# A grouped convolution, a LoRA feed-forward layer and a residual on one core: W loaded behind the first rows, shared factors cast as 96 rows, another order in the last pair

## The chip, the core and the metric

The kernel runs on one NeuronCore of a Trainium2 chip. The metric is the device time of one execution in microseconds (us); lower is better. Five engines run their own queues of instructions in order and wait for each other by semaphores: PE (matrix multiply; PEld is its weight load), DVE (elementwise, the only engine besides ACT that reads matmul results here), ACT (elementwise, casts), POOL (elementwise, in SBUF only) and SP, which here issues most of the DMAs. ACT issues the others.

## The reference

Everything is float32. Cut to what is computed, with x of 64 samples x 64 channels x 1024:

```python
# convolution over the last axis, 4 groups of 16 channels, width 9
y = conv(x, weight, pad=4, groups=4) + (cond @ c_weight.T)[:, :, None] + fside[None, :, None]
# feed-forward on rows of 1024; 8 batches, each with its own mixture of 16 LoRAs of rank 32
base  = y @ kernel + bias
A_eff = einsum('bn,nri->bri', gate, lora_A)
B_eff = einsum('bn,nor->bor', gate, lora_B)
delta = (y @ A_eff.T) @ B_eff.T + (y @ A_shared.T) @ B_shared.T
out = x + base + delta
```

## The kernel before, in words

**Precision.** PE multiplies in a reduced float32 format. Each operand is split in two: a cast on ACT gives the high part (steps whose names end in `hi`) and a subtraction gives the low part (`lo`, on DVE, or on POOL where the step carries `p`). A product is three matmuls: high x high, high x low, low x high.

**Tiles.** The 4096 rows form 16 pairs, p = 0 to 15, of 256 rows. A pair's input comes as 4 groups g (`xload p g`, 258 KB each). For pairs 0 to 2 a group is convolved by `conv` (six matmuls of 512 columns). From pair 3 on a form with fewer multiplications is used: `xdiff` (two halves), `xohi`/`xolo`, `xdhi`/`xdlo` prepare it, `convo` (3) and `convd` (6 matmuls of 256 columns) do it, `evmid` (ACT) and `evac` (DVE) take the result from PSUM. `turned` transposes it on DVE into `z`, with the rows' features on the partitions.

**Products.** Pairs 0 and 1 multiply plainly: `plain p b k` is three matmuls of output block b (2 x 2 blocks of 128 x 512) and slice k of 8. Pairs 2 to 15 use a seven-product scheme (Strassen's, in Winograd's form) on quarters of the rows and of W: `prod p j`, 12 matmuls each, for

    PRODUCTS = ((A11, B11, "a"), (A12, B21, "a"), (S1, T1, "d"), (S3, T3, "c"), (A22, N4, "c"), (S2, T2, "b"),
                (S4, B22, "d"))

The third entry is the PSUM bank in which the product is summed; there are five such banks in turn, which `fmm` and `mix` also use. `keep` (ACT) copies a bank that later products go on adding to, so the next product into that bank waits for it. `asum` (POOL) forms the sums S; `yhi`/`ylo` split an operand. `xsum`, `ysum`, `radd`, `yadd` and `total` (DVE, some on POOL) put products together with the residual rows of `rload`, and `store` writes one block of 256 KB, issued by ACT.

**W.** `wload k h` brings one of 16 pieces (256 KB, two DMAs). `fmm` multiplies the shared LoRA factors, `fadd` adds that to W, so that the shared LoRA costs the rows nothing. `whi`/`wlo` split the pieces; `wsum` forms the T and N sums for the seven-product scheme. The shared factors come by `saload`/`sbload`, 32 rows each, and are cast twice into a tile of 96 rows (two high parts, one low part: `sahi`, `salo`, `sbhi`, `sblo`).

**LoRA of a batch.** `lload`, `mix`, `mixout`, `mixput` mix the 16 factors by the gate and write them to DRAM; `aload`/`bload` read a batch's factors; `lora` multiplies a pair's rows by A, `axlow`, `axsum`, `axhi`, `axlo` split the result, and `delta` (one matmul for each block) adds B's part and the bias.

**Order.** The order of the work is written out by hand, as a long list of steps in `ORDER` (lines 50 to 246). A loop at the end of the kernel calls each step's function in that order, and each engine gets its instructions in the order in which the steps issue them; nothing reorders them later. So a step in the list sets the place of its instructions in every queue that it uses, its DMAs' place in SP's or ACT's queue too.

**Names for the lines of the profile.** L266 is any cast to a high part, L271 any subtraction for a low part; L319 is `conv`, L327 `xdiff`, L347 `convo` and `convd`, L365 `evmid`, L377/L379 `evac`, L388 `turned`, L413 `asum`, L475 `fmm`, L479 `fadd`, L485 `wsum`, L580 `plain`, L592 `prod`, L602 `lora`, L636 `keep`, L641 `xsum`, L649 `radd`, L653 `yadd`, L660 `delta`, L666 `total`, L669 `store`. In tile names `xd` is the split of a convolution's differences, `xo` that of its odd columns, `y` that of a product's operand, `wl` a low part of W, `s` a sum of `asum`, `r` the residual rows.

Of the kernel before, what the change touches and what calls it, by code (L numbers as in the profile page):

```python
# [10 lines left out]
ALU = mybir.AluOpType  # L11
# [14 lines left out]
DS = 3 * R  # L26
# [36 lines left out]
fmm 1 1, fadd 0 0, yhi 1 0, conv 2 0, wload 7 1, xlo 2 1 v, whi 0 0, fadd 0 1, biput 1, conv 2 1, whi 7 0,
fadd 1 0, wlo 0 0 p, mixput 0 0, xhi 2 2, wlo 7 0 v, mixput 0 1, whi 0 1, plain 0 0 0, fadd 1 1, xhi 2 3,
mixput 0 3, plain 0 1 0, xlo 2 2 v, whi 7 1, fmm 2 0, wlo 0 1 v, mixput 0 2, plain 0 2 0, wlo 7 1 v,
plain 0 0 1, xload 3 0, fadd 2 0, xload 3 1, fmm 2 1, plain 0 3 0, fadd 2 1, ylo 1 0 p, yhi 1 7, whi 0 2,
fmm 3 0, evac 2 0, xlo 2 3 p, whi 7 2, plain 0 3 1, wlo 0 2 v, conv 2 2, fadd 3 0, wlo 7 2 v, fmm 3 1, whi 0 3,
plain 0 0 2, fadd 3 1, plain 0 3 2, twsum, rload 0 0, whi 7 3, fmm 4 0, wlo 0 3 v, rload 0 1, plain 0 1 1,
thi 1, rload 0 2, tlo 1 v, plain 0 0 3, fadd 4 0, rload 0 3, plain 0 1 2, wlo 7 3 v, whi 1 0, fmm 4 1,
plain 0 2 1, fadd 4 1, plain 0 1 3, wsum 2 3 v, whi 6 0, plain 0 3 3, wlo 1 0 v, yhi 1 1, wlo 6 0 v, fmm 5 0,  # L70
plain 0 2 2, fadd 5 0, plain 0 1 4, ylo 1 1 v, whi 1 1, fmm 5 1, ylo 1 7 v, plain 0 0 4, aload 0, fadd 5 1,
plain 0 2 3, xohi 3 0, xdiff 3 0 0 v, whi 6 1, fmm 6 0, wlo 1 1 v, plain 0 3 4, yhi 1 4, fadd 6 0,
xdiff 3 0 1 p, plain 0 2 4, xohi 3 1, ylo 1 4 v, fmm 6 1, plain 0 0 5, fadd 6 1, xolo 3 1 p, plain 0 2 5,
wlo 6 1 v, lload 1 0, lload 1 1, lload 1 2, whi 1 2, whi 6 2, fmm 7 0, wlo 1 2 v, plain 0 3 5, wlo 6 2 v,
lload 1 3, lload 1 4, lload 1 5, lload 1 6, plain 0 2 6, fadd 7 0, xolo 3 0 p, lora 0, wsum 2 2 v, whi 1 3,
xload 3 2, wsum 2 1 v, fmm 7 1, axlow 0, turned 2 0, plain 0 1 5, evac 2 1, wsum 2 0 p, plain 0 3 6,
turned 2 1, wsum 3 0 p, conv 2 3, fadd 7 1, axsum 0, plain 0 0 6, whi 6 3, wlo 1 3 v, axhi 0, lora 1, axlo 0,
xdhi 3 0, wlo 6 3 v, lload 1 7, evac 2 2, plain 0 2 7, axlow 1, turned 2 2, wsum 3 2 p, plain 0 0 7, axsum 1,
aload 1, plain 0 1 6, total 0 0, xdlo 3 0 p, axhi 1, plain 0 3 7, evac 2 3, xdiff 3 1 0 p, plain 0 1 7,
turned 2 3, yhi 2 0, xdiff 3 1 1 p, convo 3 0, total 0 3, yhi 2 1, asum 2 3, convd 3 0, xload 3 3, evmid 3 0 a,  # L80
total 0 2, lora 2, ylo 2 1 v, xdhi 3 1, asum 2 2, xohi 3 2, evac 3 0, mix 1 0, axlow 2, xdlo 3 1 v, mix 1 1,
mixout 1 0, xdiff 3 2 0 v, mixput 1 0, mix 1 2, xdiff 3 2 1 v, mixout 1 1, turned 3 0, xolo 3 2 p, mixput 1 1,
plain 1 0 0, axsum 2, mixout 1 2, ylo 2 0 v, mix 1 3, mixput 1 2, total 0 1, plain 1 0 1, wsum 3 1 v,
xload 4 0, mixout 1 3, wsum 5 1 v, plain 1 1 0, mixput 1 3, wsum 4 1 v, plain 1 2 0, plain 1 1 1, wsum 3 3 v,
wsum 5 3 v, plain 1 3 0, wsum 4 3 v, plain 1 2 1, plain 1 1 2, wsum 5 0 v, bload 0 0, wsum 4 0 v, plain 1 2 2,
wsum 5 2 v, plain 1 3 1, bload 0 1, whi 2 0, wlo 2 0 v, whi 2 1, plain 1 1 3, wlo 2 1 v, whi 2 2, plain 1 3 2,
wlo 2 2 v, whi 2 3, plain 1 1 4, wlo 2 3 v, whi 3 0, bhi 0 0, plain 1 2 3, wsum 4 2 v, plain 1 1 5, blo 0 0 v,
bhi 0 1, plain 1 2 4, wlo 3 0 v, whi 3 1, delta 0 0 1, blo 0 1 v, plain 1 1 6, total 0 0 1, plain 1 2 5,
wlo 3 1 v, whi 3 2, store 0 0, delta 0 1 1, wlo 3 2 v, whi 3 3, plain 1 2 6, total 0 1 1, plain 1 0 2,
wlo 3 3 v, bload 1 0, whi 4 0, store 0 1, delta 0 2 1, plain 1 0 3, wlo 4 0 v, whi 4 1, plain 1 2 7,  # L90
total 0 2 1, rload 1 0, delta 0 3 1, wlo 4 1 v, whi 4 2, store 0 2, plain 1 0 4, axhi 2, total 0 3 1,
plain 1 1 7, wlo 4 2 v, store 0 3, prod 2 0, rload 1 1, whi 4 3, axlo 2, axlo 1, wlo 4 3 v, bload 1 1, whi 5 0,
rload 1 2, plain 1 0 5, yhi 2 3, rload 1 3, keep 2 0, delta 1 2 0, ylo 2 3 v, plain 1 0 6, asum 2 5,
delta 1 1 0, plain 1 0 7, total 1 1, plain 1 3 3, store 1 1, total 1 2, prod 2 3, yhi 2 2, ylo 2 2 v,
store 1 2, wlo 5 0 v, whi 5 1, asum 2 6, wlo 5 1 v, delta 1 0 0, yhi 2 4, rload 2 0, plain 1 3 4, bhi 1 0,
convo 3 1, total 1 0, whi 5 2, plain 1 3 5, rload 2 2, blo 1 0 v, store 1 0, convd 3 1, xohi 3 3, ylo 2 4 v,
keep 2 3, plain 1 3 6, xolo 3 3 v, xdhi 3 2, wlo 5 2 v, prod 2 4, evmid 3 1 a, xdlo 3 2 v, whi 5 3,
xdiff 3 3 0 v, evac 3 1, xdiff 3 3 1 p, turned 3 1, rload 2 1, xload 4 1, convo 3 2, yhi 2 5, plain 1 3 7,
evmid 3 2 a, ylo 2 5 v, convd 3 2, yhi 2 6, delta 1 3 0, xdhi 3 3, evac 3 2, convo 3 3, prod 2 1, evmid 3 3 a,
total 1 3, ylo 2 6 p, turned 3 2, store 1 3, bhi 1 1, xdlo 3 3 v, xohi 4 0, blo 1 1 v, xohi 4 1, wlo 5 3 v,  # L100
convd 3 3, yhi 3 0, xdiff 4 0 0 v, bload 2 0, prod 2 2, ylo 3 0 v, xdiff 4 0 1 v, xolo 4 0 v, rload 2 3,
xdhi 4 0, evac 3 3, xolo 4 1 p, xload 4 2, turned 3 3, prod 2 5, xdlo 4 0 v, keep 2 2, asum 3 3, yhi 3 1,
ysum 2 v, asum 3 2, ylo 3 1 v, delta 2 0, yhi 3 3, prod 2 6, total 2 0, xdiff 4 1 0 p, xsum 2, store 2 0,
xdiff 4 1 1 p, radd 2 2 v, delta 2 2, yhi 3 2, xload 4 3, convo 4 0, convd 4 0, evmid 4 0 a, radd 2 1 v,
lora 3, radd 2 3 v, xdhi 4 1, yadd 2 v, xohi 4 2, total 2 2, xolo 4 2 p, prod 3 0, rload 3 0, axlow 3,
evac 4 0, store 2 2, turned 4 0, xdlo 4 1 p, axsum 3, ylo 3 3 v, axhi 3, delta 2 1, axlo 3, delta 2 3,
asum 3 5, keep 3 0, convo 4 1, total 2 1, convd 4 1, xohi 4 3, total 2 3, store 2 1, prod 3 1, rload 3 2,
store 2 3, xdiff 4 2 0 v, xdiff 4 2 1 v, evmid 4 1 a, ylo 3 2 v, xload 5 0, xdhi 4 2, evac 4 1, xolo 4 3 p,
yhi 3 4, turned 4 1, xdlo 4 2 p, convo 4 2, yhi 3 5, ylo 3 4 v, prod 3 3, rload 3 1, evmid 4 2 a, asum 3 6,
xdiff 4 3 0 v, rload 3 3, xdiff 4 3 1 v, convd 4 2, keep 3 3, ylo 3 5 v, xload 5 1, convo 4 3, xdhi 4 3,  # L110
evac 4 2, prod 3 2, evmid 4 3 a, aload 2, turned 4 2, xdlo 4 3 p, yhi 3 6, xohi 5 0, ylo 3 6 v, xdiff 5 0 0 v,
xdiff 5 0 1 v, xohi 5 1, convd 4 3, xolo 5 0 v, keep 3 2, xolo 5 1 v, xload 5 2, prod 3 4, yhi 4 0, evac 4 3,
xdhi 5 0, turned 4 3, ysum 3 p, ylo 4 0 v, asum 4 3, xdlo 5 0 v, prod 3 5, yhi 4 1, asum 4 2, ylo 4 1 v,
# [136 lines left out]
def adaln_ffn(ctx: ExitStack, tc: tile.TileContext, xt, x, tw, w0, w1, w2, la, lb, gt,  # L250
# [164 lines left out]
    def yhi(p, b):  # L415
        if p == 1 and b in (A11, A21):
            spl[p, b] = [slot("c", f"y{q}{b}_{p}", (P, HK, P), F32R) for q in "hl"]
        else:
            t = slot("y", f"y{b}_{p}", (P, 2, HK, P), F32R)
            spl[p, b] = (t[:, 0], t[:, 1])  # L420
# [387 lines left out]
```

## Time and profile before

| | us |
|---|---|
| median of 3 runs | 467.26 (466.52 to 469.9) |
| the profiled execution, its own time | 469.12 |
| its span in the profile | 467.3 |
| busy in the span: PE / DVE / ACT / POOL | 451.1 / 415.5 / 246.2 / 213.9 |
| PEld (weight loads, beside PE) | 361.7 |

The span runs from the program's first to its last instruction; the execution's own time is 1.8 us longer. Busy times are of one engine each, and they overlap. PE's granted clock was 1.0 nearly throughout (mean 0.995). The chain of waits that ended last lies for 51% of the span on PE and for 29% on DVE. DMA engines moved 66.5 MB, at 231 GB/s in the first 10 us and 289 in the next, and at 142 over the span.

### The profile page before, as it was taken

How to read it: one execution, taken by the hardware profiler on the slowest of the kernel's cores; microseconds unless marked ns; L12 is line 12 of the kernel's file. 1: busy time of each engine (PE TensorE's matmuls, PEld its weight loads, DVE VectorE, ACT ScalarE, POOL GpSimd, SP SyncE). 2: the span in 40 equal slices, each digit the busy share in tenths (PEclk: the TensorE clock that was granted, in tenths of full speed). 3: DMA queues.
4: the chain of work that ended last, by engine and by line, in shares of the span. 5: the costliest groups of instructions: out<-in, count | busy, mean ns of one | idle time of the engine just before them, and what ended most of it. 6: DMA issues, size and time to landing. Idle time of an engine off the chain costs nothing.

```text
span 467.3 us, 7701 instructions
## 1 busy us (share of the span) xinstructions
PE 451.1 (97%) x2562; PEld 361.7 (77%) x2562; DVE 415.5 (89%) x630; ACT 246.2 (53%) x605; POOL 213.9 (46%) x181
## 2 busy tenths in 40 slices
PE   8799899999999998999999999999999999999995
PEld 7467666688888886888888888888888888888784
DVE  5799999978999879999999999998999989998734
ACT  4774354556473735556363655556363655656220
POOL 2370451022657454554546455573566553563500
PEclk9899999999999999999999999999999999999999
DMA  8999825353452625335362434335344434433232
GB/s 225 308 279 231 262 56 125 130 172 128 142 169 70 204 56 161 123 91 177 98 198 69 161 101 159 125 91 175 100 148 115 165 102 157 125 91 130 69 113 90
DMA packets 52087, 66.52 MB, mean 142 GB/s; under 512 B 6096, under 2 KB 33744, under 8 KB 52048
## 3 DMA queue, kind: packets, MB, share of 16 engines
q1 hardware_dynamic: 42112, 49.18, 36.6%
q10 hardware_dynamic: 9936, 16.86, 9.9%
q8 instruction: 20, 0.33, 0.3%
q14 instruction: 19, 0.16, 0.1%
HBM read 47.13 MB, written 18.87 MB: 141 GB/s over the span
## 4 chain that ended last, share of the span: by engine, by line
PE 51%; DVE 29%; issue 8%; DMA 5%; ACT 4%; SPq 2%; POOL 1%; DVEq 0%; ACTq 0%; POOLq 0%
PE mm_c L592 12%; PE mm_a L592 9%; PE mm_d L592 8%; PE mm_b L592 5%; PE cv L347 4%; DVE r L666 4%; DVE y L271 3%; DVE xd L271 3%; DVE xf L327 3%; DVE r L649 2%; DVE v L379 2%; PE cm L347 2%; DVE wl L271 2%; DVE bst L271 2%; PE mm_a L580 2%
## 5 line engine op out<-in xcount | busy, mean ns | idle before, releaser
L592 PE MATMUL mm_a<-wh,y 128*128 128x512 f32 x224 | 76.7, 403 | 1.4 <-ACT c L636 1.0
L592 PE MATMUL mm_d<-wh,y 128*128 128x512 f32 x224 | 75.0, 395 | 0.0
L592 PE MATMUL mm_c<-wh,y 128*128 128x512 f32 x224 | 74.8, 395 | 0.0
L266 ACT CAST y<-s 128x512 fp32r<-128x512 f32 x56 | 35.1, 626 | 67.0 <-PE mm_b L592 25.9
L271 POOL TENSOR_TENSOR xd<-xf,xd 128x512 fp32r<-128x512 f32 x21 | 27.6, 1316 | 61.8 <-ACT xd L266 61.8
L365 ACT ACTIVATE md<-cm,cadd 128x64 f32<-128x64 f32 x208 | 48.3, 317 | 12.8 <-DVE y L271 8.8
L592 PEld LDWEIGHTS mm_a<-wh,y 128*128 128x128 f32 x224 | 42.1, 188 | 13.7 <-ACT c L636 2.4
L592 PEld LDWEIGHTS mm_d<-wh,y 128*128 128x128 f32 x224 | 42.2, 188 | 9.5
L592 PEld LDWEIGHTS mm_c<-wh,y 128*128 128x128 f32 x224 | 42.0, 188 | 9.1
L388 DVE STREAM_TRANSPOSE z<-v 128x512 f32<-128x512 f32 x64 | 45.6, 712 | 2.1
L347 PE MATMUL cv<-xd,th 128*128 128x256 f32 x208 | 45.8, 282 | 1.3 <-POOL xd L271 0.8
L592 PE MATMUL mm_a<-wl,y 128*128 128x512 f32 x112 | 44.3, 396 | 0.0
L592 PE MATMUL mm_d<-wl,y 128*128 128x512 f32 x112 | 44.3, 395 | 0.0
L592 PE MATMUL mm_c<-wl,y 128*128 128x512 f32 x112 | 44.2, 395 | 0.0
L266 ACT CAST xd<-xf 128x512 fp32r<-128x512 f32 x52 | 32.6, 627 | 21.2 <-DVE xf L327 16.0
L271 DVE TENSOR_TENSOR y<-s,y 128x512 fp32r<-128x512 f32 x48 | 32.9, 686 | 11.2 <-ACT y L266 10.8
L327 DVE TENSOR_TENSOR xf<-xt 128x256 f32<-128x256 f32 x73 | 41.8, 597 | 0.8
L271 DVE TENSOR_TENSOR y<-z,y 128x512 fp32r<-128x512 f32 x38 | 40.1, 1057 | 0.9 <-ACT y L266 0.7
L266 ACT CAST y<-z 128x512 fp32r<-128x512 f32 x48 | 29.9, 623 | 18.9 <-PE mm_c L592 18.3
L413 POOL TENSOR_TENSOR s<-s,z 128x512 f32<-128x512 f32 x14 | 19.6, 1399 | 44.0 <-DVE y L271 43.0
L379 DVE TENSOR_TENSOR v<-cv,md 128x512 f32<-128x512 f32 x52 | 35.5, 683 | 4.0 <-ACT md L365 2.4
L347 PEld LDWEIGHTS cv<-xd,th 128*128 128x128 f32 x208 | 35.5, 188 | 3.3 <-DVE xd L271 1.1
(154 smaller groups left out, 1062.0 us busy)
## 6 DMA issues: line engine op xcount, KB each, us to landing
xt<-in_dram SPq DMA_DIRECT2D x64, 258.0 KB, 3.2
r<-in_dram SPq DMA_DIRECT2D x64, 256.0 KB, 3.3
out_dram<-r ACTq DMA_DIRECT2D x64, 256.0 KB, 3.4
ls<-in_dram SPq DMA_DIRECT2D x16, 256.0 KB, 5.3
br<-eff SPq DMA_DIRECT2D x48, 64.0 KB, 2.3
wr<-in_dram SPq DMA_DIRECT2D x16, 176.0 KB, 3.9
eff<-ls SPq DMA_DIRECT2D x16, 128.0 KB, 2.4
wr<-in_dram SPq DMA_DIRECT2D x16, 80.0 KB, 3.6
```

Of the source, the lines that this page charges most:

```text
L266: nc.scalar.copy(dst, src)
L271: engs[eng].tensor_tensor(dst, src, f32(hi), ALU.subtract)
L327: engs[eng].tensor_tensor(xdf[p, g][:, e], m, odd(p, g), ALU.subtract)
L347: nc.tensor.matmul(ps, a[:, w, g, :], b, start=(n == 0), stop=(n == 2))
L365: nc.scalar.activation(t[:, n], cpm[p, g][:, n], ACTF.Identity, bias=c[:, n:n + 1])
L379: nc.vector.tensor_tensor(v.rearrange("p n (i e) -> p e n i", e=2), cps.pop((p, g)), mid.pop((p, g)).unsqueeze(1).to_broadcast([P, 2, 4, H ...
L388: nc.vector.transpose(z[:, :, :, :, gg, :], vs.pop((p, g)).rearrange("p m j -> p (m j)"))
L413: engs[eng].tensor_tensor(t, m, n, op)
L580: nc.tensor.matmul(acc[p, BLOCKS[b]], m[:, kk, :], n, start=(k == 0 and q == 0), stop=(k == 7 and q == 2))
L592: nc.tensor.matmul(ps, a[:, k, :], b[bb, k], start=s, stop=(k == HK - 1 and q == 2), skip_group_check=not first)
L649: engs[eng].tensor_tensor(r, r, cop[p, "x"], ALU.add)
L666: nc.vector.tensor_tensor(r, acc[p, (BLOCKS[b], b)[of]], r, ALU.add)
```

## The change

- **Front of the order.** One of the two tap loads, pair 0's rows and the shared factors are loaded first, then W's first piece, pair 1's and most of pair 2's rows, and the rest of W. All LoRA loads (`lload`) move behind W, and `mix` behind the start of pair 0's products. Pair 0's products start after pair 0's convolutions and the first two of pair 1; before, they started after those of pairs 0 and 1 and two of pair 2. Three evacuations (`evac 0 0`, `1 0`, `1 3`) go from DVE to ACT.
- **Shared factors.** The host lays them out three times over 96 rows in both kernels. Before, 32 of these rows were loaded and cast twice; now all 96 are loaded (192 KB instead of 64) and cast by one instruction, and the low part is taken from rows of the same partitions.
- **Pairs.** Among the steps on DVE and POOL, 16 `xdiff`, 19 `xdlo`, 18 `xolo` and 3 `ysum` (net, of the whole kernel) go from POOL to DVE, and 15 `ylo` from DVE to POOL. `lora` of the next pair and its first product now come ahead of the following pair's first convolution, and each group's convolution shifts accordingly.
- **Last pair.** Its products go 0, 2, 1, 5, 3, 4, 6 instead of 0, 3, 1, 2, 4, 5, 6. Block 1, which is last, is totalled in two halves of 256 columns (`totalh`), which are stored by SP and by ACT (`storeh`).
- `yhi` gets a condition on PLAIN, which is 2 in both.

The number and shape of PE's instructions stay the same. The diff, with the list of steps cut to its beginning and end:

```diff
 ORDER = """
-twload 0, gload, warm, busy 22, twload 1, cwload, xload 0 0, ctload, xload 0 1, small 0, xload 0 2, small 1,
-xload 0 3, lload 0 0, lload 0 1, thi 0, saload 0, sbload 0, tlo 0 v, thi 2, saload 1, cwide, sbload 1, tlo 2 v,
-lload 0 2, xhi 0 0, cmul, lload 0 3, xlo 0 0 v, xload 1 0, xhi 0 1, gmask, xload 1 1, conv 0 0, xload 1 2,
-csum, bihi, xload 1 3, xlo 0 1 v, biput 0, evac 0 0, xhi 0 2, conv 0 1, lload 0 4, lload 0 5, turned 0 0,
...
+warm, twload 0, small 0, busy 22, xload 0 0, gload, twload 1, cwload, xload 0 1, ctload, saload 0, small 1,
+sbload 0, saload 1, sbload 1, thi 0, xload 0 2, xload 0 3, tlo 0 v, xhi 0 0, wload 0 0, xlo 0 0 v, thi 2,
+wload 0 1, cwide, xload 1 0, tlo 2 v, xhi 0 1, cmul, xload 1 1, xlo 0 1 v, xload 1 2, sahi 0, conv 0 0, gmask,
+xload 1 3, sbhi 0, xload 2 0, csum, sahi 1, xload 2 1, salo 0 v, conv 0 1, xload 2 2, sbhi 1, sblo 0 v,
+wload 1 0, bihi, salo 1 v, evac 0 0 a, fmm 0 0, wload 1 1, sblo 1 v, xhi 0 2, turned 0 0, wload 2 0, fmm 0 1,
...
-yhi 15 5, ylo 15 5 v, rload 15 1, rload 15 3, prod 15 2, yhi 15 6, ylo 15 6 v, prod 15 4, keep 15 2, ysum 15 v,
-prod 15 5, delta 15 0, xsum 15, prod 15 6, total 15 0, radd 15 1 v, store 15 0, radd 15 3 v, radd 15 2 v,
-delta 15 2, delta 15 1, yadd 15 v, delta 15 3, total 15 2, total 15 1, store 15 2, total 15 3, store 15 1,
-store 15 3
+yhi 15 4, ylo 15 4 v, rload 15 2, rload 15 3, prod 15 5, yhi 15 6, ylo 15 6 v, delta 15 0, xsum 15, prod 15 3,
+total 15 0, radd 15 1 v, store 15 0, radd 15 2 v, radd 15 3 v, delta 15 3, keep 15 3, delta 15 1, prod 15 4,
+ysum 15 v, yadd 15 v, total 15 3, store 15 3, prod 15 6, delta 15 2, totalh 15 1 0, total 15 2, storeh 15 1 0,
+totalh 15 1 1, store 15 2, storeh 15 1 1
 """

     def yhi(p, b):
-        if p == 1 and b in (A11, A21):
+        if PLAIN == 2 and p == 1 and b in (A11, A21):

     def saload(h):
-        sar[h] = piece(f"sar{h}", (R, HN))
-        nc.sync.dma_start(sar[h], las[0:R, HN * h:HN * h + HN])
+        sar[h] = piece(f"sar{h}", (DS, HN))
+        nc.sync.dma_start(sar[h], las[:, HN * h:HN * h + HN])

     def sahi(h):
         sa[h] = piece(f"sa{h}", (DS, HN), F32R)
-        hi_of(sa[h][0:R], sar[h])
-        hi_of(sa[h][R:2 * R], sar[h])
+        hi_of(sa[h], sar[h])

     def salo(h, eng="v"):
-        engs[eng].tensor_tensor(sa[h][2 * R:3 * R], sar[h], f32(sa[h][0:R]), ALU.subtract)
+        d = sa[h][2 * R:3 * R]
+        lo_of(d, sar[h][2 * R:3 * R], d, eng)
...
+    def totalh(p, b, c):
+        s = slice(c * HN // 2, (c + 1) * HN // 2)
+        r = res[p, b][:, s]
+        nc.vector.tensor_tensor(r, acc[p, BLOCKS[b]][:, s], r, ALU.add)
+
+    def storeh(p, b, c):
+        n = HN // 2
+        (nc.sync, nc.scalar)[c].dma_start(xrow(out, p, b)[:, :, c * n:c * n + n], res[p, b][:, c * n:c * n + n])
```

`sbload`, `sbhi` and `sblo` change as `saload`, `sahi` and `salo` do.

## The prediction

> **What bounds the kernel now.** I read the totals first (PE is busy 451.1 us of a 467.3 us span), then busy time by stage. The four stages run from the first convolution (7.1 us) to pair 1's first product (72.1), to pair 3's first (124.5), through eleven alike pairs (to 415.7), and to the last matmul.
>
> ```profile
> core 0: us, PE busy (x) PEld busy (x) DVE busy (x) ACT busy (x) POOL busy (x), PEclk, DMA share, GB/s
> 7.10:72.10 65.00, 59.14 (x320) 39.69 (x319) 60.29 (x91) 36.83 (x72) 29.74 (x23) 0.97 0.78 224
> 72.10:124.50 52.40, 51.66 (x265) 40.65 (x263) 47.12 (x74) 27.02 (x60) 10.75 (x9) 1.00 0.48 143
> 124.50:415.70 291.20, 288.50 (x1721) 238.75 (x1717) 273.46 (x410) 161.66 (x428) 158.00 (x132) 1.00 0.42 130
> 415.70:461.70 46.00, 46.00 (x241) 37.20 (x237) 30.35 (x51) 17.39 (x42) 14.41 (x11) 1.00 0.28 97
> ```
>
> PE looks full, but its ends are modelled, so I count what it issues. The chain of waits prices the pieces: 2.80 us for a product's 12 matmuls (0.233 each), 0.35 and 0.71 for the two parts of a late convolution, 1.01 for a `lora`.
>
> ```profile
> 253.13 2.81 PE mm_d L592 x12
> 255.94 0.23 PE mm_c L660
> 256.17 0.35 PE cm L347 x3
> 256.52 0.71 PE cv L347 x6
> 257.23 1.01 PE axp L602 x32
> ```
>
> A pair is 7 x 2.80 + 4 x 1.06 + 4 x 0.233 + 1.01 = 25.75 us. Stage 3 is 11 pairs, 283.3 us of work in 291.2: 7.9 lost. Stage 1 holds 12 first-form convolutions (1.40 each), 16 `fmm` (0.235), 7 `mix` (0.96), 3 `lora`, 32 `plain` (0.70) and one late convolution: 53.7 us in 65.0, so 11.3 lost. Stage 2 loses 1.9, stage 4 0.3. So 21 us of issue time are to be had, over half at the front.
>
> Third, rows by form on DVE and POOL, to see who makes PE wait.
>
> ```profile
> L327 DVE TENSOR_TENSOR xf<-xt 128x256 f32<-128x256 f32 x73 | 41.8, 597 | 0.8
> L271 DVE TENSOR_TENSOR y<-z,y 128x512 fp32r<-128x512 f32 x38 | 40.1, 1057 | 0.9 <-ACT y L266 0.7
> ...
> L271 DVE TENSOR_TENSOR y<-s,y 128x512 fp32r<-128x512 f32 x48 | 32.9, 686 | 11.2 <-ACT y L266 10.8
> ...
> L271 DVE TENSOR_TENSOR xd<-xf,xd x31: 648/725/1822, 70.3 to 424.2; 128x512 fp32r<-128x512 f32 x31
> L271 POOL TENSOR_TENSOR xd<-xf,xd x21: 1272/1302/1527, 63.6 to 427.8; 128x512 fp32r<-128x512 f32 x21
> ```
>
> The last two lines give shortest, median and longest. The same subtraction takes DVE 0.65 us or up to 1.82, and the difference is about one POOL operation (1.3). Over their shortest, five groups lose 50 us: `xf` 12, `y<-z` 15, `xd` 15, `wl` 5, the first `r` addition 3. That is about 0.25 us per us of POOL's 213.9. The Trainium skill (SBUF — State Buffer, Who interferes with whom) says that a DVE operation with two SBUF inputs and a GpSimd one that reads SBUF hold a shared port in turn, and the loser waits in full.
>
> **The change, part by part.** DVE steps are counted at their back-to-back spacing: 0.60 us for 128x512 (three radds in 1.89), 0.635 for a transpose, 0.335 for 256 columns, 0.55 for an `axsum`.
>
> *Front.* Ahead of pair 0's first product, DVE had 24 full steps, 8 transposes, 3 short ones and the mask (0.46) = 21.0 us of work, and the product began at 32.2: 11.2 us above its work. Now it has 17, 4, 2 and the mask = 13.9, since pair 1's convolutions follow the first W. DVE cannot begin before its first loaded data (5.1), so the product begins between 19.0 and 25.1. I take 21.9, the 8.0 between. The first W tile now stands behind 2.3 MB on SP instead of 4.4; at the 231 GB/s that moved in the first 10 us and the 289 in the next, plus 2.4 us to land, it is there near 13.5 instead of 20.4. The last W (9.0 MB deep) is in by 36 and is needed after 50. `saload`/`sbload` carry 192 KB for 64 and pass groups 2 and 3 of pair 0's rows, which now end 2.05 and 2.31 MB deep: they land near 11.3 and 12.4 us instead of 8 and 9. Bare, that is 3.4 us; the bounds on the start contain it. Eight ACT casts become four (2.5 us less), but all four wait for the wider loads, and `evac 0 0` (0.95 us on ACT for 0.6 on DVE) and the next `xhi` queue behind them: the value 8.0 rather than 5.1.
>
> From there to pair 1's first product DVE had 33.2 us of work and took 39.9, with 17.5 us of POOL beside it. Now it has 39.0 (pair 0's T and N sums come forward) with 11.6 us of POOL: 4.4 us extra in proportion, 6.7 if it stays, 5.0 taken. So 21.9 + 39.0 + 5.0 = 65.9. PE's work up to there is 48.3 (two `lora`, one `mix` and two convolutions later), so it loses 65.9 - 7.1 - 48.3 = 10.5, against 11.3: **gain 0.8**, from -4.1 (start 25.1, extra 6.7) to +4.3 (start 19.0, extra 4.4).
>
> *Stage 2.* PE has 54.9 us, DVE 42.0 plus at most 6: PE sets it. The named gaps of before are two single-bank `delta` waits and two of 0.28 behind `mix`; the same bank pattern stays, and `mix` now also takes turns with `fmm` in the spare bank. Loss 0.5 to 2.5, taken 1.5 against 1.9: **gain 0.4**. `aload 0` and eight `mixput` issues move behind W; the `lora 0` that needs them waits behind 32 products.
>
> *Pairs.* 32 steps net leave POOL in these 11 pairs: 11 `xdiff`, 18 `xdlo`, 13 `xolo`, 3 `ysum` go to DVE and 13 `ylo` come. POOL falls by 29 us to 129; DVE rises from 215.1 to 253 x 0.60 + 44 x 0.635 + 122 x 0.335 + 11 x 0.55 = 226.7. With 0.25 per POOL us: 254.6 before, 259.0 after, under PE's 283.3. The rows thus say +4.4 on DVE, hidden by 2.2 us of slack per pair. By the skill's exclusive lock alone each POOL us removed could free up to one, 29 - 11.6, and DVE would fall by 17.
>
> The gaps of before that are named are few:
>
> ```profile
> PE mm_a L592 <- ACT c L636: 1.0, 2, 0.8
> ...
> PE cv L347 <- POOL xd L271: 0.8, 1, 0.8
> ```
>
> Both sit at 180-183, where a convolution waited for POOL's `xdlo` and the next product for `keep`. With `xdlo` on DVE that goes, but later `xdlo` now queue behind `evac` and the transpose, 1 us before the convolution needs them: one POOL collision (1.2 us) is late. **Gain 1.5**, from -5 (0.5 more per pair) to +5.
>
> *End.* PE's last issue is at 461.51, the last store lands 4.8 us later: three totals, three issues, three blocks on one queue.
>
> ```profile
> 463.03 0.68 DVE L666 TENSOR_TENSOR r<-mm_b,r 128x512 f32<-128x512 f32 x1
> ...
> 462.55 1.88 ACTq L669 DMA_DIRECT2D out_dram<-r  x3
> ...
> out_dram<-r ACTq DMA_DIRECT2D x4, 256.0 KB, 2.5
> ```
>
> Now one `delta` follows the last product, then half (0.41, as the 128x256 `cadd`), total, half. Counting from the last issue: first half done 0.6, total 1.2, second half 1.55. SP issues the first half; ACT issues block 2 at 1.25 and the last half at 1.85. It lands at 4.0 (less than 2.5 later, half the bytes) to 4.35: 0.45 to 0.8 saved. The Trainium skill (DMA: Bandwidth & Descriptors, Issuing engines are not separate DMA queues) speaks against more: a second queue saves only issue time. With its 2.0 us per DMA plus bytes at 436 GB/s the halving would be worth 0.3 us. The new order costs something: only two `delta` (0.47) stand between S3·T3 and A22·N4, while `keep 3` starts 0.39 after the last matmul's issue and takes 0.59 and up to 0.15 of signals, against 0.23 + 0.47 of PE: 0.4 us. **Gain 0.3** (-0.2 to 0.8).
>
> The condition added in `yhi` always holds, as PLAIN is 2, and costs nothing. Sum: 0.8 + 0.4 + 1.5 + 0.3 = 3.0. The profiled execution took 469.12 us for its 467.3 span and would become 466.1; the median of the three runs is 467.26, so 3.0 less is 464.3, **464**.
>
> **Rivals.** *Slower: DVE becomes the bound of the pairs.* Place: `xdlo`, `xolo`, `xdiff` among the evacuations. It decides once a POOL us costs DVE (283.3 - 226.7) / 129 = 0.44 us. Against it: 0.25 now. For it: 0.38 per POOL us with all waits in the W stage, and DVE is already busy 273 of 291. At 0.5, a pair needs 26.5, plus the 0.7 that a pair loses today, so 0.8 more in each of 12: 467.3 + 9.6 - 1.5 = 475. *Faster: the waits go.* The start is at its floor (4.3), stage 2 and pairs lose what can't be helped (1.4 + 5), the end 0.3: 11 less, 456; three quarters of that give 459. For it: the idle is real, and POOL's late `xdlo` leaves. *The front brings nothing*, because DVE, not W, held it: 467.
>
> **Numbers.** My forecast 0.45 (own range 461 to 467.5), faster rival 0.25, front without effect 0.1, slower rival 0.2. Within 1% (462.6 to 471.9) is what a measurement can't tell from no change. Faster: 0.25 x 0.95 + 0.45 x 0.3 = 0.37. Slower: 0.2. Same: 0.43. The range 457 to 473 leaves out the far ends of both rivals.
>
> **What would show it.** Right: the first `plain` near 22 us and pair 1's near 66; POOL near 175 us busy; `xd` on DVE about 50 times; last landing 4.0 to 4.4 us after PE's last issue; a 0.4 us PE gap at `keep 3`. Wrong: pair spacing over 26.5 us with DVE over 97% busy, or a PE wait on ACT's `sb` casts past 15 us.

## The result, and the profile after

| | before | after |
|---|---|---|
| median, us (runs) | 467.31 (4) | 522.42 (4) |
| profiled execution, its own time / span | 469.12 / 467.3 | 522.44 / 520.7 |
| mean granted clock of PE | 0.995 | 0.959 |
| busy: PE / DVE / ACT / POOL | 451.1 / 415.5 / 246.2 / 213.9 | 472.6 / 452.7 / 244.0 / 184.5 |

The ratio is 1.116 (95% interval 1.111 to 1.121): 55 us slower, where I had forecast 464, in a range from 457 to 473.

Busy time by stage after, cut at the same points of PE's work as before (first convolution, pair 1's first product, pair 3's, pair 14's, last matmul; columns as before):

```profile
8.55:69.50 60.95, 55.68 (x237) 35.41 (x236) 57.59 (x87) 29.74 (x60) 15.80 (x12) 0.97 0.81 241
69.50:131.75 62.25, 58.22 (x340) 44.50 (x336) 50.63 (x78) 31.76 (x73) 15.81 (x12) 0.97 0.39 117
131.75:463.68 331.93, 302.40 (x1721) 247.64 (x1717) 302.50 (x442) 160.10 (x429) 140.73 (x101) 0.95 0.37 114
463.68:515.67 51.99, 49.14 (x249) 39.55 (x246) 37.49 (x59) 18.04 (x47) 11.13 (x8) 0.97 0.29 96
```

Against before, pair 3 starts 7.3 us later, the eleven pairs take 40.7 us more (331.9 for 291.2), the end 6.2 more, and the span ends 0.8 us sooner after PE's last issue (5.0 for 5.8): 53.4, the difference of the spans. Three quarters lie in the pairs, where DVE's busy time rose by 29 us although POOL's fell by 17.

Who made PE wait, after (total us, times, longest):

```profile
PE mm_a L594 <- ACT c L638: 32.2, 12, 3.5
PE dl L662 <- DVE bst L272: 2.5, 1, 2.5
...
PE cv L348 <- DVE xd L272: 1.4, 2, 0.9
```

Before, the first of these was 1.0 us in 2 waits. Now it comes once in each pair from 3 to 14: the second product goes on adding to bank a and waits for `keep 0`, ACT's copy of that bank. The chain of waits in pair 10 says what `keep 0` waits for (start, us, what; lines have moved by one or two):

```profile
338.97 0.04 DVE r L651
339.01 1.61 issue
340.62 3.48 DVE r L651 x2
...
344.19 0.10 DVE r L655
344.29 1.42 issue
345.71 0.68 DVE r L668
346.39 0.19 DVE axs L617
...
347.01 0.40 ACT axt L267
...
347.86 0.59 ACT c L638
348.46 0.04 issue
348.50 3.69 PE mm_a L594 x8
```

Read it upwards: the product (348.50) waits for the copy (`c`), the copy stands on ACT behind `axhi` (`axt`), that waits for `axsum` (`axs`) on DVE, and that stands behind a `total`, `yadd` (L655) and three `radd` (L651), which take 5.1 us where three take 1.9 alone. DVE's rows by operation, after, and the same row before:

```profile
L651 DVE TENSOR_TENSOR r<-r,c 128x512 f32<-128x512 f32 x42 | 60.4, 1489 | 0.4
L655 DVE TENSOR_TENSOR r<-r,c 128x512 f32<-128x512 f32 x14 | 19.4, 1384 | 0.6
```
```profile
L649 DVE TENSOR_TENSOR r<-r,c 128x512 f32<-128x512 f32 x42 | 31.1, 794 | 0.4
```

And what POOL does at that time (timeline of POOL after, from 335.88):

```profile
335.88 1.58 POOL L414 TENSOR_TENSOR s<-z,z 128x512 f32<-128x512 f32 x1 [0.28 <-DVE z L389]
337.42 1.48 POOL L414 TENSOR_TENSOR s<-z 128x512 f32<-128x512 f32 x1
338.86 1.29 POOL L272 TENSOR_TENSOR y<-s,y 128x512 fp32r<-128x512 f32 x1
340.23 1.61 POOL L414 TENSOR_TENSOR s<-s,z 128x512 f32<-128x512 f32 x1
341.80 1.73 POOL L272 TENSOR_TENSOR y<-s,y 128x512 fp32r<-128x512 f32 x1
343.61 1.62 POOL L414 TENSOR_TENSOR s<-z,s 128x512 f32<-128x512 f32 x1
```

Six operations without a gap. Of the 42 `radd`, 34 run more than 70% of their time beside POOL and take 1.65 us on average; the 6 that run alone take 0.68. DVE operations that read PSUM are untouched: the totals of bank a take 0.677 beside POOL and 0.686 alone, the evacuations 0.692 and 0.687; transposes (one input) 0.711 and 0.713. The Trainium skill (SBUF — State Buffer, Who interferes with whom) says just this: a DVE instruction with at most one SBUF input, outside the modes that use two ports, doesn't contend with GpSimd. The trace agrees, and I had used the page's other half only.

Last, the clock: 10 times in pairs 3 to 14, after such a wait, PE runs at half clock for 3.41 us. PE's account of a pair closes with that: 25.75 us of work, 2.7 of wait for `keep 0` (32.2 / 12) and 1.4 lost to the clock are 29.8 of the 30.1 that a pair takes.

### The profile page after: what moved, and what is told of

Read it like the earlier page. It is cut to its first block, busy times and chain, and to the rows that moved or that the text cites. A ratio compares the mean times of both kernels' runs of the same rounds, so it can differ in the third digit from the quotient of the medians.

```text
span 520.7 us, 7639 instructions
## 1 busy us (share of the span) xinstructions
PE 472.6 (91%) x2562; PEld 373.6 (72%) x2562; DVE 452.7 (87%) x671; ACT 244.0 (47%) x613; POOL 184.5 (35%) x138
## 4 chain that ended last, share of the span: by engine, by line
PE 47%; DVE 32%; issue 11%; ACT 5%; DMA 3%; SPq 1%; POOL 0%; DVEq 0%; ACTq 0%
PE mm_a L594 12%; PE mm_c L594 11%; DVE r L651 7%; PE mm_d L594 6%; DVE y L272 4%; PE cv L348 4%; DVE r L668 3%; DVE xd L272 3%; DVE v L380 3%; DVE z L389 2%; PE cm L348 2%; PE mm_a L582 2%; PE mm_d L582 2%; PE mm_b L594 2%; PE mm_b L582 2%
## 5 line engine op out<-in xcount | busy, mean ns | idle before, releaser
L594 PE MATMUL mm_a<-wh,y 128*128 128x512 f32 x224 | 88.4, 459 | 32.2 <-ACT c L638 32.2
L594 PEld LDWEIGHTS mm_a<-wh,y 128*128 128x128 f32 x224 | 49.4, 221 | 48.2 <-ACT c L638 34.6
L651 DVE TENSOR_TENSOR r<-r,c 128x512 f32<-128x512 f32 x42 | 60.4, 1489 | 0.4
L594 PE MATMUL mm_a<-wl,y 128*128 128x512 f32 x112 | 50.4, 450 | 0.0
L328 DVE TENSOR_TENSOR xf<-xt 128x256 f32<-128x256 f32 x89 | 46.2, 548 | 1.5
L272 POOL TENSOR_TENSOR y<-s,y 128x512 fp32r<-128x512 f32 x25 | 36.7, 1466 | 22.6 <-ACT y L267 22.6
L267 ACT CAST axt<-axs 32x256 fp32r<-32x256 f32 x32 | 12.9, 404 | 62.7 <-DVE axs L617 62.3
L272 DVE TENSOR_TENSOR xd<-xf,xd 128x512 fp32r<-128x512 f32 x50 | 39.4, 789 | 0.1
L594 PE MATMUL mm_b<-wh,y 128*128 128x512 f32 x112 | 37.4, 395 | 0.0
```

The lines of the kernel that those rows point to most:

```text
L267: nc.scalar.copy(dst, src)
L272: engs[eng].tensor_tensor(dst, src, f32(hi), ALU.subtract)
L328: engs[eng].tensor_tensor(xdf[p, g][:, e], m, odd(p, g), ALU.subtract)
L594: nc.tensor.matmul(ps, a[:, k, :], b[bb, k], start=s, stop=(k == HK - 1 and q == 2), skip_group_check=not first)
L651: engs[eng].tensor_tensor(r, r, cop[p, "x"], ALU.add)
```

## The experiments

Steps are shown for one pair; each edit does the same in pairs 3 to 15 or 3 to 14. The kernel before ran beside each group, at 467.2 to 468.2.

**e1: `keep 0` ahead of `axhi`.**

```diff
-axsum 9, ylo 9 3 p, store 8 2, xdiff 10 1 0 v, axhi 9, asum 9 5, axlo 9, delta 8 1, keep 9 0,
+axsum 9, ylo 9 3 p, store 8 2, xdiff 10 1 0 v, keep 9 0, axhi 9, asum 9 5, axlo 9, delta 8 1,
```

> The kernel after, with keep 0 of pairs 3 to 15 (the copy of bank a on ACT) moved ahead of the pair's axhi in ACT's queue; nothing else moves, DVE's and POOL's queues are the same. Theory W (a chain of waits: PE's second product into bank a waits for keep 0, which stands on ACT behind axhi, which waits for axsum on DVE, which stands behind radd and yadd that POOL slows; each gap of PE of about 2.8 us is followed by 3.4 us at half clock): the twelve waits of 32.2 us in all go, and with them 12 x 1.7 us of slow clock, so 522.4 - 32 - 20 = 470, between 464 and 482; the mean clock is back at 0.99; radd stays near 1.4 us. Rival D (DVE, with the work that left POOL, sets the pace of a pair): PE waits somewhere else for the same time, 512 to 522, clock still 0.96.

Measured: 510.2 (ratio 1.092, 1.088 to 1.095). That lies just below D's range and far from W's, but the chain in the same pair shows that the edit missed its aim (21.6 us of waits for `keep 0` are left):

```profile
339.64 0.68 DVE r L668
340.31 0.19 DVE axs L617
...
340.81 0.08 ACTq L671
340.89 0.04 issue
340.93 0.59 ACT c L638
```

`ACTq L671` is a `store`. ACT issues it, it waits for `total 2` on DVE, and `keep 0` stands behind it: the copy still waits for the slow additions.

**e2: `axsum` earlier on DVE.**

```diff
-radd 8 2 v, lora 9, radd 8 3 v, prod 9 0, yadd 8 v, axlow 9, total 8 2, rload 9 0, axsum 9,
+radd 8 2 v, lora 9, axlow 9, axsum 9, radd 8 3 v, prod 9 0, yadd 8 v, total 8 2, rload 9 0,
```

> The kernel after, with axlow and axsum of pairs 3 to 15 ahead of the third radd, yadd and a total of the pair before (where before they came behind them), so that DVE reaches axsum some 3 us earlier; ACT's order of axhi and keep 0 stays. Theory W: axhi ends before the first product does, keep 0 finds ACT free and the twelve waits go: 470, between 464 and 482, as in the run with keep 0 first, with radd still slow beside POOL (about 1.4 us). Rival D: the same number of DVE instructions in another order, 512 to 522.

Measured: 527.2 (1.130, 1.125 to 1.134), a miss for both, and slower than after. PE's waits for `keep 0` grew from 32.2 to 37.1 us: `axsum` is early, but `total 2` and with it the `store` ahead of `keep 0` on ACT are later. It says again that the `store` matters, and no more.

**e3: two of POOL's steps to DVE.**

```diff
-ylo 9 3 p, store 8 2, xdiff 10 1 0 v, axhi 9, asum 9 5,
+ylo 9 3 v, store 8 2, xdiff 10 1 0 v, axhi 9, asum 9 5 v,
```

> The kernel after, with two steps of pairs 3 to 14 moved from POOL to DVE: asum 5 and ylo 3, which stood on POOL beside radd and yadd. Order of the list unchanged. DVE gets 24 more operations of 0.6 us (14.4 us), POOL's chain beside radd is cut in two. Theory W: radd falls from 1.49 us to below 1.0, axsum comes 2 to 3 us earlier, most of the twelve waits and the slow clock go: 468 to 488. Rival D: DVE has 14 us more to do, 530 to 540.

Measured: 482.5 (1.033, 1.031 to 1.036). DVE got 24 operations more, its busy time fell from 452.7 to 435.2, and 40 us went. Its row:

```profile
L651 DVE TENSOR_TENSOR r<-r,c 128x512 f32<-128x512 f32 x42 | 31.6, 807 | 0.4
```

A DVE that simply has too many instructions can't do this. POOL beside them is the cause of the slow additions. This run doesn't tell place from quantity, since POOL's work fell too, by 3.4 us a pair.

**e4: the gap filled.** Twelve matmuls of 512 columns ahead of the second product:

```diff
+    def fill(p):
+        t = acc[p, "c"] = pmm.tile([P, HN], F32, tag="mm", name=f"mm{p}_c")
+        for _ in range(12):
+            nc.tensor.matmul(t, th[:, 0, 0, :], th[:, 0], start=True, stop=True)
```

> The kernel after, with twelve matmuls of 512 columns (2.8 us at 0.233 each) put into PE's queue just ahead of the second product of pairs 3 to 14; they write a bank that the next product overwrites, use constant operands and are no part of the result. They fill the gap in which PE waits for keep 0, so that the gap's length stays in the time while PE does not stand idle. Theory W (the slow clock comes from the idle gap): only the slow clock goes, 522.4 - 12 x 1.7 = 502, between 496 and 508, mean clock 0.99. Rival C (the lower clock has another cause, such as heat or the load of the whole kernel): 518 to 530 and a mean clock near 0.96.

Measured: 512.2 (1.097, 1.095 to 1.100), mean clock 0.988; no half-clock stretch is left in the pairs. C falls: the slow clock follows the idle gap. Half of what I expected came, for reasons that can be counted: 10 stretches, not 12, give 10 x 1.7 = 17; the filling is 33.6 us for gaps of 32.2; and waits for `keep 0` and for `xd` of 4.6 us more appear behind it. 17 - 1.4 - 4.6 = 11, for 10.3 measured. This is an account from the trace, not a further test.

**e5: `keep 0` ahead of the `store` too.**

```diff
-prod 9 0, yadd 8 v, axlow 9, total 8 2, rload 9 0, axsum 9, ylo 9 3 p, store 8 2,
+prod 9 0, yadd 8 v, axlow 9, keep 9 0, total 8 2, rload 9 0, axsum 9, ylo 9 3 p, store 8 2,
```

> The kernel after, with keep 0 of pairs 3 to 15 ahead of the store of the pair before as well as of axhi in ACT's queue (directly behind axlow); DVE's and POOL's queues unchanged. In the run with keep 0 first, the chain shows ACT's store waiting for total 2, which stands on DVE behind the slow radd and yadd, so keep 0 was still behind DVE. Theory W (what costs the time is that PE's next product waits, by way of ACT's queue, for DVE's slowed additions): now nothing of DVE stands ahead of keep 0, the waits at the second product go and with them the slow clock: 468 to 484, radd still at 1.4 to 1.5 us. Rival D (DVE's additions, slowed by POOL, set the pace of the pair whatever waits for them): PE waits elsewhere, for the convolutions' operands above all, 498 to 512.

Measured: 504.3 (1.079, 1.074 to 1.083), in D's range. The waits for `keep 0` are gone, all of them, and PE waits for the next thing:

```profile
PE cm L348 <- ACT md L366: 10.1, 11, 1.9
PE cv L348 <- DVE xd L272: 5.5, 11, 0.9
PE cv L348 <- ACT xd L267: 4.1, 6, 1.1
```

`md` is `evmid`, which stands on ACT behind the same `store` and `axhi`. Theory W, one chain that a better queue order cuts, falls. DVE's lateness reaches PE by whichever hand-over comes next.

**e9: POOL's chain later.** No instruction changes its engine:

```diff
-asum 9 2, yhi 9 3, total 8 0, xsum 8,
+asum 9 2, total 8 0, xsum 8,
...
-axsum 9, ylo 9 3 p, store 8 2, xdiff 10 1 0 v, axhi 9, asum 9 5, axlo 9, delta 8 1, keep 9 0,
+axsum 9, store 8 2, xdiff 10 1 0 v, axhi 9, axlo 9, delta 8 1, keep 9 0, yhi 9 3, ylo 9 3 p, asum 9 5,
```

> The kernel after, with yhi 3, ylo 3 and asum 5 of pairs 3 to 14 moved behind keep 0 in the list. The same instructions on the same engines, DVE and PE in the same order; POOL, whose queue has ylo 3 and what follows behind that cast, now starts this part of its chain some 4 us later, after the additions radd and yadd. Theory P (place: POOL costs DVE time only beside operations with two inputs in SBUF, and beside radd and yadd this time reaches PE): radd falls below 0.9 us, the waits for keep 0 go, 470 to 482 with the front's 7 us still in it. Rival Q (quantity: it is the total of POOL's work that slows DVE, wherever it stands): radd's loss turns up at other operations, 500 or more.

Measured: 513.9 (1.099, 1.094 to 1.103). All 42 `radd` run alone now, and DVE's next operations with two SBUF inputs pay instead (timeline of DVE, pair 10):

```profile
336.84 1.89 DVE L651 TENSOR_TENSOR r<-r,c 128x512 f32<-128x512 f32 x3
...
346.14 2.84 DVE L328 TENSOR_TENSOR xf<-xt 128x256 f32<-128x256 f32 x2
348.90 1.51 DVE L272 TENSOR_TENSOR xo<-xt,xo 128x256 fp32r<-128x256 f32 x1
```

Two `xf` take 0.76 alone, an `xo` 0.42: 3.2 us are lost here where `radd` and `yadd` lost 4.1. So theory P, that only the additions are a bad place, fell: a closed chain of POOL operations costs DVE about 1 us for each operation with two SBUF inputs that it meets, and these `xf` and `xo`, which the next convolution needs, are on the path too. Rival Q was right here in number, but quantity isn't all either, as the kernel before shows with more POOL work and less loss.

**e12: the reverse, in the kernel before.** Six POOL operations of 128x256 on constants beside `radd`:

```diff
-xdiff 10 1 0 p, xohi 10 2,
+xdiff 10 1 0 p, spin, spin, spin, spin, spin, spin, xohi 10 2,
...
+        nc.gpsimd.tensor_tensor(scratch[0], f32(th[:, 0, 0:2]), f32(tl[:, 0, 0:2]), ALU.add)
```

> The kernel before, with six more POOL operations of 128x256 for each of pairs 3 to 14 (two constant inputs in SBUF, a scratch tile as output, no part of the result), placed in POOL's queue behind xdiff 1, where radd and yadd run on DVE. It puts into the kernel before what the change is said to have done. Theory P: radd's mean rises from 0.79 to 1.1 us or more, PE waits for keep 0 or for a convolution's operands, and the time rises by 1 to 2.5 us in each of 12 pairs: 480 to 498. Rival S (DVE, which is idle for some 50 us of the span, has room for it): below 473, with radd slow all the same.

Measured: 497.8 (1.063, 1.059 to 1.068), theory P's upper end, with `radd` just short of the 1.1 us that it asked for. Work for which nobody waits costs 30 us:

```profile
L653 DVE TENSOR_TENSOR r<-r,c 128x512 f32<-128x512 f32 x42 | 41.8, 1046 | 0.4
```

**e6 and e15: order or engines?** e6 is after's order with before's engines for `xdiff`, `xdlo`, `xolo`, `ysum` and `ylo` from pair 3 on; e15 is before's order with after's engines.

> The kernel after, with its order of steps, but from pair 3's first product on each xdiff, xdlo, xolo, ysum and ylo on the engine that it had before (110 steps go back). Theory E (it is the exchange of ylo for xd and xo steps that puts POOL beside the additions): radd falls below 1.0 us, the waits for keep 0 mostly go, 472 to 488. Rival O (it is the order: lora and the first product of a pair come a convolution earlier, and POOL's sums with them): radd stays above 1.2 us and the time above 495.

> The kernel before, in its own order, but from pair 3's first product on with xdiff, xdlo, xolo, ysum and ylo on the engines of after (108 steps change). With the run of after's order on before's engines (496.9) it makes the table of two by two. DVE's undisturbed work rises by 1.2 us for each pair (20.7 to 21.9), POOL's falls by 1.6. If the order of the pairs alone brings POOL beside the additions: loss stays near 0.29 us per POOL us, 21.9 + 3.7 = 25.6 in a pair, PE's 25.75 still bounds it: 466 to 474. If the engines bring it, in either order: radd above 1.1 us, DVE at 27 us for a pair, 480 to 495.

Measured: e6 496.9 (1.062, 1.058 to 1.065), of which the front is 7: rival O's time, with `radd` at 1.01 us between the two theories. e15 is 514.4 (1.101, 1.098 to 1.103), more than either theory gave it. Taking the front out (475.0, below), the pairs cost 22 us by the order alone, 47 by the engines alone and 47 by both. The engines suffice; the order by itself costs too, but the two don't add (47 with both, not 69). Why the engines bring POOL together is seen on POOL's timeline, first before, then in e15, each from a pair's first `asum`:

```profile
275.78 1.58 POOL L413 TENSOR_TENSOR s<-z,z 128x512 f32<-128x512 f32 x1 [2.94 <-DVE z L388]
277.32 1.73 POOL L413 TENSOR_TENSOR s<-z 128x512 f32<-128x512 f32 x1
279.02 1.74 POOL L271 TENSOR_TENSOR y<-z,y 128x512 fp32r<-128x512 f32 x1
280.71 0.61 POOL L327 TENSOR_TENSOR xf<-xt 128x256 f32<-128x256 f32 x1
283.88 0.74 POOL L271 TENSOR_TENSOR xo<-xt,xo 128x256 fp32r<-128x256 f32 x1 [2.56 <-ACT xo L266]
285.86 1.31 POOL L271 TENSOR_TENSOR xd<-xf,xd 128x512 fp32r<-128x512 f32 x1 [1.23 <-ACT xd L266]
288.12 1.51 POOL L413 TENSOR_TENSOR s<-s,z 128x512 f32<-128x512 f32 x1 [0.95 <-DMA xt<-in_dram]
```
```profile
323.07 1.57 POOL L413 TENSOR_TENSOR s<-z,z 128x512 f32<-128x512 f32 x1 [0.33 <-DVE z L388]
324.60 1.73 POOL L413 TENSOR_TENSOR s<-z 128x512 f32<-128x512 f32 x1
...
327.83 1.29 POOL L271 TENSOR_TENSOR y<-s,y 128x512 fp32r<-128x512 f32 x1 [0.25 <-ACT y L266]
329.20 1.36 POOL L413 TENSOR_TENSOR s<-s,z 128x512 f32<-128x512 f32 x1
330.89 1.70 POOL L271 TENSOR_TENSOR y<-s,y 128x512 fp32r<-128x512 f32 x1 [0.33 <-DVE xf L327]
```

Before, `xo` and `xd` on POOL wait for ACT's casts (2.56 and 1.23 us idle), and just then, at 280.8 to 283.8, DVE does its three `radd` and `yadd`. In e15 these steps are on DVE, `ylo` steps whose casts are done have taken their place, and POOL runs straight on into the additions. It is so beyond this pair: of the 30 `radd` in the ten pairs, none runs more than 70% of its time beside POOL before, 20 do in e15 and 28 in after. That the waiting steps were spacers, which kept POOL's work apart, is my reading of this; no run moves them alone.

DVE's time for one pair, worked out from each trace over ten pairs (pair 4's first product to pair 14's). Loss is what an operation takes beyond its undisturbed 0.685 us (128x512), 0.713 (transpose) or 0.42 (256 columns); idle is DVE's empty time; work is the rest. Lost to the clock is PE's:

| us per pair | pair | work | loss | idle | POOL busy | loss per POOL us | clock |
|---|---|---|---|---|---|---|---|
| before | 26.5 | 20.7 | 4.2 | 1.7 | 14.4 | 0.29 | 0 |
| after | 30.1 | 21.9 | 5.7 | 2.6 | 12.8 | 0.44 | 1.4 |
| e3 | 26.9 | 23.1 | 3.1 | 0.8 | 9.4 | 0.33 | 0 |
| e6 | 28.2 | 20.6 | 4.6 | 3.0 | 14.9 | 0.31 | 0.3 |
| e9 | 29.4 | 21.8 | 4.8 | 2.8 | 12.2 | 0.39 | 0.7 |
| e12 | 28.6 | 20.7 | 5.8 | 2.1 | 20.6 | 0.28 | 0 |
| e15 | 30.5 | 21.6 | 5.6 | 3.2 | 12.6 | 0.45 | 1.5 |

PE needs 25.75. After and e15 have 27.5 and 27.2 of work and loss: DVE is the bound. That its idle time is added because PE, late and slow, is late for DVE in turn is argued, not tested. In e6 work and loss are 25.2, less than PE's; there the loss costs by its place, ahead of a hand-over (10 waits for `keep 0`, 12.7 us, are left). Before, after and e6 show that the rate isn't fixed: with after's order and before's engines (e6), POOL is busy longest of the three (14.9 us), at a rate of 0.31. e12, at 0.28, doesn't tell place from quantity; it shows that more POOL work beside `radd` is enough to make DVE the bound (26.5).

**e7, e10 and e14: the front.** e7 is after's order up to pair 3's first product, then before's. e10 and e14 start from it:

```diff
-wlo 3 3 v, plain 1 0 3, plain 1 1 3, bload 1 0, whi 4 0, wlo 4 0 v, whi 4 1, wlo 4 1 v, whi 4 2,
-plain 1 2 3, wlo 4 2 v, bhi 0 0, plain 1 3 3, whi 4 3, blo 0 0 v, plain 1 0 4, wlo 4 3 v, bload 1 1, bhi 0 1,
+wlo 3 3 v, bhi 0 0, blo 0 0 v, bhi 0 1, blo 0 1 v, plain 1 0 3, plain 1 1 3, bload 1 0, whi 4 0, wlo 4 0 v,
+whi 4 1, wlo 4 1 v, whi 4 2, plain 1 2 3, wlo 4 2 v, plain 1 3 3, whi 4 3, plain 1 0 4, wlo 4 3 v, bload 1 1,
```

In e14, `whi 4`, `wlo 4`, `whi 5` and `wlo 5` stand behind pair 0's totals besides.

> The order after up to pair 3's first product, with its 96-row factors and W behind the first rows, and from there the remaining steps in the order and on the engines of before. It measures the front alone. In the profiles pair 3's first product begins at 124.5 us before and at 131.8 after. If these 7.3 us are the front's own and are not made up later: 474.5, between 472.5 and 476.5. If the pairs behind it take part of it back, or were late in the profile after because of them: below 471.

> The kernel with the front after and the pairs of before (475.0), with the casts and subtractions of batch 0's B factors (bhi 0 0, blo 0 0, bhi 0 1, blo 0 1) ahead of the splits of W's pieces 4 and 5 in ACT's and DVE's queues instead of among them. Theory F (a third of the front's 7.3 us is the 2.7 us in which PE waits for the first delta, with the slow clock behind it): the wait falls to under 0.6 us, 471 to 473.5. Rival (the factors' DMAs are late, or the splits that now wait behind make a new wait): 474 to 477.

> The kernel with the front after and the pairs of before (475.0), with batch 0's B factors ahead of the splits of W's pieces 4 and 5 as in the run with B factors first, and these splits now behind the four totals of pair 0 instead of ahead of them. In that run the wait went from the first delta (2.6 us) to the second, for a total that stood on DVE behind the splits (3.0 us). Theory F (5 of the front's 7.3 us are DVE's lump of W's splits ahead of what PE waits for, and the slow clock after it): both waits under 0.6 us, 469 to 472. Rival (the splits are needed there, and their products wait instead): 474 or more.

Measured: e7 475.0 (1.015, 1.012 to 1.019), as expected; e10 477.3 (1.019, 1.014 to 1.024), at the end of the rival's range; e14 471.9 (1.009, 1.007 to 1.011). In e10 the wait had only changed its place, from the first `delta`'s B factors to the second's bank, which a `total` behind the splits had to free:

```profile
PE dl L662 <- DVE r L668: 3.0, 1, 3.0
```

In e14 two waits of a `dl` are left, 0.7 and 0.4 us, and 3 of the front's 7 us are back: about half by the shorter wait, half by the half-clock stretch that followed it in e7 (87.3 us) and is gone. What costs the other 4 I haven't separated; among PE's waits in e14 are 1.8 us for `wr` near 23 us, 1.3 for an `fmm` near 59, 0.5 and 0.9 for `xd` near 114 and 119, and the first convolution is 0.6 to 1.4 us later in the runs with this front.

**e11: e9 and e10 together on after.**

> The kernel after with both edits: POOL's chain behind keep 0, and batch 0's B factors ahead of the splits. Theories P and F together: 3 us less than the run with POOL's chain later alone, 467 to 479; PE's named waits all under 1.5 us from pair 3 on. Rival Q: 497 or more.

Measured: 513.7 (1.098, 1.094 to 1.101), nothing on top of e9, as both had failed alone.

**e8, e13 and e16: the other parts alone, in the kernel before.** e8 has the last pair's order and half stores, e13 the 96-row factors, e16 both.

> The kernel before, with only the last pair's products in the new order and its last block in two halves stored by SP and ACT. In the profile after, the last product waits 0.37 us longer for keep 3, and the span ends 5.0 us after PE's last issue instead of 5.8. My step of the prediction said a gain of 0.3 (from -0.2 to 0.8); the profile after says 0.4: 466.8, between 466.2 and 467.4. Rival (the second queue and the halves save nothing, the wait stays): 467.6 or more.

> The kernel before, in its own order, with only the shared factors loaded and cast as 96 rows (192 KB for 64, four ACT casts for eight). Theory: the factors are needed by the first shared product only at 27.8 us, so neither the four casts saved (2.5 us of ACT) nor the 128 KB more on SP are on the path: 466.3 to 468.5. Rival (the wider loads, ahead of the first rows on SP, delay pair 0's convolutions): 468.5 to 470.

> The kernel before, in its own order, with the 96-row factors and with the new last pair and stores (0.998 of before alone). If both parts are free of the pairs: 465.8 to 467.2, a ratio of 0.995 to 0.999. If either costs something in company: 1.000 or more.

Measured: e8 467.1 against 468.2 beside it (0.998, 0.996 to 1.000); e13 465.3 (0.996, 0.994 to 0.998); e16 464.9 (0.995, 0.993 to 0.997), the lowest time of this study. The last pair's part can't be told from no change: e8's interval reaches 1.000, and e16's overlaps e13's. e13 beat its expectation, by ACT's rows for `sahi`, before and in e13:

```profile
L266 ACT CAST sa<-sar 32x512 fp32r<-32x512 f32 x4 | 2.5, 618 | 1.4 <-DMA sar<-in_dram 1.3
```
```profile
L266 ACT CAST sa<-sar 96x512 fp32r<-96x512 f32 x2 | 1.2, 620 | 1.0 <-DMA sar<-in_dram 1.0
```

A cast of 96 rows takes as long as one of 32. Before, the eight casts stood from 12.1 to 17.2 us ahead of pair 1's first `xhi`, for which PE waited 2.3 us, with a half-clock stretch behind it (19.0 to 22.4). In e13 the casts end at 14.5, that stretch is gone, pair 0's first product begins at 29.7 for 32.2, and pair 3 keeps the gain (121.8 for 124.5). My expectation looked at who needs the factors, not at what stands behind them on ACT.

## Why the prediction was wrong

**Pairs: the step that failed** is "with 0.25 per POOL us: 254.6 before, 259.0 after, under PE's 283.3", 2.2 us of slack for each pair. DVE's own work I had right (1.1 us more a pair; measured 1.2). The rate I carried over as if it were a property of POOL's work, where it is one of its place. Before, 42% of POOL's time in the pairs (4 to 13) lay beside DVE operations with at most one SBUF input, the totals, evacuations and transposes, which it doesn't slow; after, 22%, in e15, 17%; the rows that I read showed all five slowed groups and that `radd` was hardly among them, and I didn't ask why. With the exchange, 0.29 became 0.44 us per POOL us: in ten pairs, work and loss on DVE are 27.5 us a pair where I had 23.5 (259.0 / 11) and PE needs 25.75. So 1.5 gained became 40.7 lost, with 5.7 in pair 14. POOL's term was too small as well: it is busy 140.7 us in the eleven pairs, not 129, because its own operations got longer beside DVE (`s<-s,z` 1.40 to 1.61 us, `y<-s,y` 1.29 to 1.47). The order of the pairs, for which I allowed at most 5 us, costs 22 by itself (e6). Behind that stand two steps that I left out: what waits for DVE when it is late (`keep 0`, by way of `axhi` and a `store` in ACT's queue; the prediction prices nothing in that queue), and the clock, whose 10 stretches lose PE 17 us (e4, which fills the gaps, gets 10 back). Of the signs that I had named, the 50 `xd` on DVE came, POOL stayed above its 175 us (184.5), and the sign against me came, a pair over 26.5 us; only DVE's share, 91% in the pairs (302.5 of 331.9), stayed below the 97% that I had asked for, since DVE waits for PE too.

**The slower rival** named the mechanism, that DVE becomes the bound, and its point, 0.44. That the profile after stands at that number is in part luck: with the POOL time measured, 140.7 us, the point is (283.3 - 226.7) / 140.7 = 0.40, and after is past it. It put the place at `xdlo`, `xolo` and `xdiff`, priced it at 475 and got a chance of 0.2. It too held the rate for a constant that needed no cause to change.

**Front: right to the first product, wrong behind it.** I had 21.9 us for pair 0's first product; it is 20.6. I had 65.9 for pair 1's; it is 69.5. In stage 2 I took 1.5 us of loss, since "the same bank pattern stays"; it is 62.25 - 54.9 = 7.4. The new order casts batch 0's B factors behind W's splits of pieces 2, 3 and most of 4 on ACT and DVE, before only behind piece 2 and the start of 3; I had looked at what waits for `aload`, not for `bload`. e7 puts the front at 7 us; e14 shows 3 of them to be this wait and the half clock behind it.

**End: right in the profile.** `keep 3` makes PE wait 0.37 us (0.4 predicted), and the last landing comes 4.0 us after PE's last issue (4.0 to 4.35). A gain of 0.3 us is too small for the times to confirm (e8). **96 rows: half right.** The 2.5 us of ACT were counted, but set off against wider loads; alone the part is worth 2 us.

## What to carry to other kernels

Before you move work between DVE and POOL, write down what stands beside each POOL operation: beside DVE operations that read PSUM or have one input it costs nothing, beside those with two SBUF inputs about 1 us each here, and POOL steps that wait for something may be the pauses in which such operations run. Then ask who waits for DVE if it is late, a `store` in a queue of casts included. Splitting this change would have given the 0.5% of e16 without the 12% of the whole.

## What the runs showed of the hardware

- Beside back-to-back POOL operations of 1.3 to 1.7 us, a DVE addition of 128x512 with two SBUF inputs takes 1.65 us on average for 0.68 (34 `radd` in after); beside e12's shorter ones of 0.99, it takes 1.11.
- PE's half clock needs no long gap. Its stretches of 3.41 us begin whole multiples of 3.41 us apart (140.34 and 171.06 in after: 9 x 3.41). Measured from issue to issue, gaps of 2.9 to 3.8 us in after are all followed by one, of two gaps of 2.7 only one is (at 406.5, not at 228.2); in e1 gaps of 2.06 us are followed by one at 339.5 and 455.7 and by none at 165.2 and 369.1, a gap of 3.2 us at 426.5 isn't followed by one either, and in e12 gaps up to 2.6 us never are. Where a gap lies between those multiples decides most of it. Cut the 18 traces, from 30 us to PE's last issue, into windows of 3.41 us at the multiples: of the windows at full clock, all 43 in which PE is idle for more than 1.9 us are followed by a half-clock window, 18 of the 33 with 1.6 to 1.9 us are, and none of the 2223 with less. So 2.4 idle us in one window at 406.5 bring the half clock; the same at 228.2, split 0.6 and 1.8 over two windows, don't. Why those between 1.6 and 1.9 go either way isn't settled. The Trainium skill (TensorE: Matmul & The Clock Gate, Part 1) tells of a free-running window of 3.4 us, which agrees with the spacing, and of an idle window of that length before the clock falls, which these gaps and windows undercut.
- A cast on ACT of 96 rows by 512 takes 0.62 us, as one of 32 rows.
